# Four outer products of the squares in one joint tree: a bilinear kernel with a planned order

## The chip, the cores and the metric

The kernel runs on one core of a Trainium2 chip. The metric is the device time of one execution in microseconds (us), as the median of several runs. The core's engines work side by side and wait for each other by semaphores: TensorE (PE: matmuls from SBUF into PSUM), VectorE (DVE), ScalarE (ACT), GpSimd (POOL) and SyncE (SP, here only a queue for DMAs). ACT and POOL issue DMAs too; those that add onto their destination are POOL's.

## The reference

With x of 1024 x 512 and 64 embeddings, all in float32:

```python
out_lin = x @ lin_w.T + lin_b
xv = jnp.einsum('bf,efm->bem', x, weight)
zp = jnp.einsum('bf,efm->bem', jnp.square(x), jnp.square(weight))
y = out_lin + 0.5 * jnp.sum(jnp.square(xv) - zp, axis=1)
```

The sum over e of the second einsum is one product, of the squares of x (1024 x 512) with the squares of the weights summed over e (512 x 512).

## The kernel before, in words

**Tiling.** The model's 512 columns are worked in 16 groups of 32 (`group(g)`). A group is a product of x with a 512 x 2048 block of weights (32 columns times 64 embeddings). It is done by Strassen's scheme in Winograd's form on two levels: seven outer products (`ORDER`), each a `tree` of seven inner products. A product (`product`, L623) is two matmuls of 128x512 into the two banks of a PSUM tile. The inner sums of the weights (`t1` to `t4`) are POOL's; the outer sums T1 and T2 are built in memory, by a plain load and accumulating loads on POOL (`outer_sum`, `load_more`, L559). Of each tree, ACT copies three intermediate results out of PSUM or between PSUM tiles, DVE adds (L310), ACT squares (L324), DVE sums over the embeddings (L331). Outer product 4 is the sixth of a group and 3 the seventh; the text calls them tree 4 and tree 3. PSUM has four tiles of two banks: `b1`, `b3`, `b2_0`, `b2_1`.

**The squares.** The squares of x are made in groups 1 to 7 and parked in memory (`sq_dram`), with the sums of the inner level for outer products 1, 2, 5 and 6; the summed squares of the weights (`w2_sum`) grow with every group. Their product is made at the end: outer products 1, 2, 5 and 6 in inner trees, 7, 3 and 4 directly (`one_level`, L1083: the left operands are the plain loads raw7, raw3 and raw4). Its quarters go to the buffers v, o2, u2 and f, which are 256 columns wide in each of four positions.

- `twin_tree` makes two outer products side by side, one in each bank of a PSUM tile, with matmuls of 256 columns (L938). `first_twins` sets 1 and 2 ahead of tree 4 of the last group; the second pair, 6 and 5, is set behind tree 3.
- `preload` copies a sum of SBUF into a bank (ACT, L322), `one_level` adds a product onto it, `collect` adds the bank to one of the four blocks of the result (DVE, L1095). The blocks l11, l12, l21 and l22 hold the linear part, loaded by `lin_load` with accumulating loads of the interaction (L851).
- `add_to` (L824) adds v and o2 to l11 by accumulating DMAs on POOL. `turn` and `place` bring the last group's sums into rows (oa2), which `add_edge` adds to the result. `store` (L1036) writes the result, on SP's or ACT's queue, as the planner chooses.

**The order.** Nothing is issued as it is written: `Plan.add` records each step with its costs, reads and writes, and `Plan.order` emits all of them by a list schedule. TensorE's steps follow a fixed order by key (7 times the tree's number plus `PLACE`, so that neighbouring trees interleave); the others are taken by their latest times, with assumed costs, a hop of 0.3 us between engines and 0.05 on the same one. The names `b1`, `b3`, `b2_0`, `b2_1` stand for two banks each (`PAIRS`), which can be handed on one by one.

Of the kernel before, what the change touches and what calls it, by code (L numbers as in the profile page):

```python
# [29 lines left out]
class Plan:  # L30
# [11 lines left out]
    PAIRS = ("b1", "b3", "b2_0", "b2_1")  # L42
# [6 lines left out]
    def add(self, costs, emit, reads=(), writes=(), key=None, land=0.0,  # L49
# [7 lines left out]
            [m for n in names for m in (((n, 0), (n, 1)) if n in self.PAIRS else (n,))]  # L57
            for names in (reads, writes)
        )
        for r in reads:  # L60
            if r in self.writer:
                op.deps.add(self.writer[r])
# [11 lines left out]
    def order(self):  # L74
# [34 lines left out]
        def ready(o, e=None):  # L109
            at = self.HOP  # L110
            for d in o.deps:
                own = ops[d].engine == e and not ops[d].move
                at = max(at, ops[d].end + (self.OWN if own else self.HOP))
            return at
# [82 lines left out]
def kernel(  # L197
# [139 lines left out]
    def dma(o, i, reads, writes, move=1.75):  # L337
        plan.add({SP: 0.45}, lambda _: nc.sync.dma_start(o, i), reads, writes, land=2.0, move=move)
# [379 lines left out]
    def place(dst, b, names, writes, move):  # L718

        rows = dst.rearrange("m (n q b) -> q m n b", q=P // MG, b=MG)  # L720
        for q in range(P // MG):
            dma(rows[q], buf["turned"][ts(q, MG), b, :], names, (writes + (q,),), move)
# [78 lines left out]
    S = 7 * NG + 1  # L801
# [31 lines left out]

    def square_load(i):

        names = (f"R{i}", f"X{i}", f"Y{i}")
        dma(buf[f"X{i}"], sq_dram[:, i - 1], (("sqd", i),), names, 3.1)
# [84 lines left out]
    def twin_tree(at, b2, members):  # L922


        bank = {n: buf[n][:, :, 0:Q] for n in ("b1", "b3", b2)}
        side = {}
        for p, c in ((5, 0), (3, 1)):
            n = "wsq_1", c
            side[p] = buf["wsq_1"][:, c].rearrange("p (u b) -> p u b", u=2), n
            used("wsq_1", n, (n, 0), (n, 1))  # L930
        raw = all(src is None for _, src, _ in members)

        def product(p, b, first):
            for u, (i, _, _) in enumerate(members):
                op, names = tt[i][p]
                plan.add(
                    {PE: PAIR / 4},
                    lambda _, u=u, i=i, op=op: nc.tensor.matmul(  # L938
                        bank[b][:, u], op, buf[f"X{i}"][:, SLOT[p], :], start=first, stop=True,
                        skip_group_check=True,  # L940
                    ),
                    names + (f"{'Y' if p == 7 else 'X'}{i}", (b, u)), ((b, u),),
                    key=7 * at + PLACE[p] + 0.1 * u,
                )

        def aside(p, pos):
            o, n = side[p]
            act(o, bank["b3"], None, ("b3",), ((n, 0), (n, 1)), 0.65)
            for u, (_, src, _) in enumerate(members):
                if src:  # L950
                    costs, emit = two_input(POOL, o[:, u], o[:, u], part(src, pos), False, Q)
                    plan.add(costs, emit, ((n, u), (src, pos)), ((n, u),))

        def to(pos, b, p=None):

            if raw:
                q, c = divmod(pos, 2)
                o = buf[members[0][2][0]][:, :, c, ts(q, Q)]
                writes = tuple((dst, pos) for _, _, dst in members)
                if p is None:  # L960
                    act(o, bank[b], None, (b,), writes, 0.65)
                else:
                    plan.add(
                        {DVE: 0.62}, lambda _: nc.vector.tensor_add(o, bank[b], side[p][0]),
                        (b, (side[p][1], 0), (side[p][1], 1)), writes,
                    )
                return
            for u, (_, src, dst) in enumerate(members):
                if src is None and p is None:
                    act(part(dst, pos), bank[b][:, u], None, ((b, u),), ((dst, pos),), 0.4)  # L970
                    continue
                o, n = (side[p][0][:, u], (side[p][1], u)) if p else (part(src, pos), (src, pos))
                plan.add(
                    {DVE: 0.36},
                    lambda _, u=u, o=o, dst=dst: nc.vector.tensor_add(  # L975
                        part(dst, pos), bank[b][:, u], o
                    ),
                    ((b, u), n), ((dst, pos),),
                )

        product(5, "b3", True)
        aside(5, 3)
        product(3, "b3", False)
        aside(3, 1)
        product(1, "b1", True)
        act(bank[b2], bank["b1"], None, ("b1",), (b2,), 0.65)
        product(6, b2, False)
        to(1, b2, 3)
# [3 lines left out]
        to(3, b2, 5)  # L992
# [6 lines left out]
    def first_twins():  # L999
        halves_of(w(NG, "w22"))  # L1000
        halves_of("w12")
        lin_load(0, 0)
        for c in range(2):
            for z in range(2):
                halve(c, z)
        square_load(1)
        square_load(2)
        tt_at = w(NG, "w22"), 1
        w2_inner((1, 2), w2_sum.rearrange("p (r k) m -> p r k m", r=2)[:, :, :, 0:HM],
                 [("w2h", r, 0) for r in range(2)], tt_at,  # L1010
                 buf[tt_at].rearrange("p a n -> p (a n)"), *parts(tt_at))
# [4 lines left out]
        halves_of("T2")  # L1016
        used(*parts(tt_at), *((tt_at, "t", k, z) for k in range(1, 5) for z in range(2)))
        for block in ((1, 1), (0, 1), (1, 0)):
            lin_load(*block)
# [4 lines left out]
    def store(h, c, pos):  # L1024
# [10 lines left out]
        plan.add(  # L1035
            {SP: 0.45, ACT: 0.45}, lambda e: queues[e].dma_start(d, o),  # L1036
            tuple((n, z) for z in pos), (), land=2.0, move=0.44 * len(pos),
        )
# [17 lines left out]
    group(last, {5: first_twins})  # L1056


    raw = {}
    for i in (7, 3, 4):  # L1060
        n, at = f"raw{i}", {7: 7, 3: 1, 4: 2}[i]
        buf[n], raw[i] = block4(at), n
        used(f"X{at}", f"R{at}", f"Y{at}", n)
        dma(buf[n], sq_dram[:, i - 1, 0:4, :].rearrange("p (k q) b -> p k (q b)", k=2),
            (("sqd", i),), (n,))
    right = {7: (t_all[:, 2], "zt", 3), 4: (t_all[:, 3], "zt", 4), 3: (quad[1, 1], "w2h", 1, 1)}

    def bank_ap(bank):
        return buf[bank] if bank in buf else buf[bank[0]][:, bank[1], :]

    def preload(bank, src, u, lo, hi):
        here = tuple((src, pos) for pos in range(4) if pos % 2 == u and lo <= pos // 2 * Q < hi)
        act(bank_ap(bank)[:, 0:hi - lo], buf[src][:, u, lo:hi], None, here, (bank,),
            0.12 + 0.22 * (hi - lo) / Q)

    def one_level(i, bank, u, lo, hi, key):

        ap, *name = right[i]
        o = bank_ap(bank)[:, 0:hi - lo]

        def emit(_):
            for k in range(KH):
                nc.tensor.matmul(  # L1083
                    o, ap[:, k, ts(u, P)], buf[raw[i]][:, k, lo:hi], start=False, stop=k == 1,
                    skip_group_check=True,
# [5 lines left out]
    def collect(block, bank, u, lo, hi):  # L1091
        n = lin_all[block]
        here = tuple((n, pos) for pos in range(4) if pos % 2 == u and lo <= pos // 2 * Q < hi)
        d, o = buf[n][:, u, lo:hi], bank_ap(bank)[:, 0:hi - lo]
        plan.add({DVE: 0.08 + 0.28 * (hi - lo) / Q}, lambda _: nc.vector.tensor_add(d, d, o),  # L1095
                 here + (bank,), here)
        return here

    halves_of("T1")
    used("w11", *(("zt", k, z) for k in range(1, 5) for z in range(2)))  # L1100
    for z in range(2):
        w2_outer(z)
    w2_inner((5, 6), t_all[:, 0:2], [("zt", k) for k in (1, 2)], "wsq_0",
             buf["wsq_0"].rearrange("p a n -> p (a n)"))
    for i in (6, 5):
        square_load(i)
    b2 = b2_ring()
    upper = {u: (b2, u, "upper") for u in range(2)}
    for u, n in upper.items():
        buf[n] = buf[b2][:, u, Q:N]  # L1110
        used((b2, u), n)
    for q in range(2):
        for u in range(2):
            preload(upper[u], l21, u, q * Q, (q + 1) * Q)
            one_level(4, upper[u], u, q * Q, (q + 1) * Q, ((-0.6, -0.4), (9.5, 6.4))[q][u])
            act(part(l21, 2 * q + u), buf[upper[u]], None, (upper[u],), ((l21, 2 * q + u),), 0.34)
# [5 lines left out]
    for pos in (1, 3, 0, 2):  # L1122
        for o, a, b in ((v, u2, f), (l22, l22, f)):
            costs, emit = two_input(POOL, part(o, pos), part(a, pos), part(b, pos), False, Q)
            plan.add(costs, emit, ((a, pos), (b, pos)), ((o, pos),))
# [56 lines left out]
```

## Time and profile before

| | |
|---|---|
| median of 3 runs | 1409.11 us (1408.74 to 1409.27) |
| profiled execution, its own time | 1409.28 us |
| its span, first to last instruction | 1407.2 us |
| PE busy | 1398.1 us |
| DVE busy | 1094.7 us |
| POOL busy | 1043.1 us |
| ACT busy | 711.8 us |
| granted TensorE clock | 1.0 |

Times in the profile's rows are microseconds from the start of the span, means in the groups are nanoseconds. "Idle before" is how long an engine stood still ahead of a row, with what ended the wait. Each float32 matmul stands as two records, so a product of two matmuls is "x4". TensorE's ends are modelled; start to start is the safer reading. A DMA's row tells when it was issued; its landing stands apart, in the lists of DMAs.

### The profile page before, as it was taken

To read this page: it belongs to the slowest core of one execution; us is meant where nothing else is said; L and a number is where in the kernel's file an instruction comes from. 1 tells how busy PE (TensorE), PEld (TensorE's weight loads), DVE (VectorE), ACT (ScalarE), POOL (GpSimd) and SP (SyncE) were. 2 spreads that over 40 slices of the span, in tenths; PEclk is the share of its full clock that TensorE was granted. 3 is DMA by queue.
4 is the path that set the end of the run, shared out by engine and by line. 5 is a ranking of instruction groups with operands and counts; after the bars stand their busy time and mean duration, and the time that the engine had idled before them with its cause. 6 is when DMAs were issued, how large, how long until landed. Compare 5 with 4: busy or idle time off the path is not lost.

```text
span 1407.2 us, 10698 instructions
## 1 busy us (share of the span) xinstructions
PE 1398.1 (99%) x3308; PEld 628.9 (45%) x3308; DVE 1094.7 (78%) x976; ACT 711.8 (51%) x760; POOL 1043.1 (74%) x736
## 2 busy tenths in 40 slices
PE   9999999999999999999999999999999999999997
PEld 5444444444444444444444444444444444444454
DVE  7978696867969787795967869687795968869566
ACT  4545463544736456463544636454463644637334
POOL 5696776958678696776958678686777868679784
PEclk9999999999999999999999999999999999999999
DMA  6573564917649283573808447282663808447464
GB/s 224 165 190 120 134 183 116 249 53 189 214 106 236 88 226 125 146 213 101 221 30 197 135 116 187 60 241 61 159 174 90 213 30 208 125 120 183 107 177 108
DMA packets 55286, 211.84 MB, mean 151 GB/s; under 512 B 21504, under 2 KB 23296, under 8 KB 33344
## 3 DMA queue, kind: packets, MB, share of 16 engines
q0 software_dynamic: 12464, 83.76, 30.6%
q1 hardware_dynamic: 41200, 125.71, 25.2%
q10 hardware_dynamic: 1568, 1.71, 0.3%
q8 instruction: 27, 0.44, 0.1%
q14 instruction: 27, 0.22, 0.0%
HBM read 180.75 MB, written 12.45 MB: 137 GB/s over the span
## 4 chain that ended last, share of the span: by engine, by line
PE 98%; DMA 1%; DVE 0%; ACT 0%; issue 0%; ACTq 0%; SPq 0%; DVEq 0%
PE b L623 96%; PE b L456 1%; PE b L938 1%; PE b L1083 1%; DMA oa<-xT 0%; DMA ob<-lin_wT 0%; ACT b L322 0%; DVE T L975 0%; DVE w22a L1095 0%; ACT T L322 0%; DVE x_all L310 0%; ACTq L356 0%; DVE T L1095 0%; SPq L349 0%; ACT ob L324 0%
## 5 line engine op out<-in xcount | busy, mean ns | idle before, releaser
L623 PE MATMUL b<-t,x_all 128*128 128x512 f32 x1792 | 806.2, 592 | 0.0
L623 PEld LDWEIGHTS b<-t,x_all 128*128 128x128 f32 x1792 | 340.5, 190 | 425.6 <-issue 419.5
L623 PE MATMUL b<-w,x_all 128*128 128x512 f32 x768 | 358.1, 592 | 0.0
L310 POOL TENSOR_TENSOR t<-w 128x512 f32<-128x512 f32 x128 | 174.3, 1362 | 154.8 <-PE b L623 85.0
L322 ACT COPY p<-b 128x1024 f32<-128x1024 f32 x161 | 161.8, 1005 | 159.6 <-PE b L623 159.5
L623 PEld LDWEIGHTS b<-w,x_all 128*128 128x128 f32 x768 | 145.9, 190 | 182.9 <-issue 171.7
L310 POOL TENSOR_TENSOR t<-w,t 128x512 f32<-128x512 f32 x128 | 176.4, 1378 | 60.4 <-PE b L623 60.4
L324 ACT ACTIVATE oa<-oa 128x1024 f32<-128x1024 f32 x124 | 129.7, 1057 | 142.6 <-DVE oa L310 142.5
L623 PE MATMUL b<-T,x_all 128*128 128x512 f32 x384 | 180.4, 592 | 0.0
L331 DVE TENSOR_REDUCE acc<-oa 128x16 f32<-128x1024 f32 x124 | 148.9, 1211 | 37.9 <-ACT oa L324 37.9
L322 ACT COPY b<-b 128x1024 f32<-128x1024 f32 (+1 forms) x114 | 113.0, 992 | 119.8 <-PE b L623 119.4
L331 DVE TENSOR_REDUCE w_sum<-wsq 128x16 f32<-128x1024 f32 x128 | 154.1, 1206 | 12.5 <-ACT wsq L324 12.5
L310 DVE TENSOR_TENSOR oa<-b,p 128x1024 f32<-128x1024 f32 x95 | 115.8, 1219 | 38.9 <-PE b L623 38.8
L324 ACT ACTIVATE wsq<-w 128x1024 f32<-128x1024 f32 x96 | 98.2, 1056 | 67.8 <-DVE w_sum L331 67.8
L310 POOL TENSOR_TENSOR t<-T 128x512 f32<-128x512 f32 x64 | 90.3, 1411 | 56.6 <-issue 33.2
L324 ACT ACTIVATE c<-c 128x1024 f32<-128x1024 f32 x77 | 79.4, 1057 | 77.5 <-POOL c L310 51.7
L623 PEld LDWEIGHTS b<-T,x_all 128*128 128x128 f32 x384 | 73.0, 190 | 91.8 <-issue 91.6
L310 DVE TENSOR_TENSOR p<-b,p 128x1024 f32<-128x1024 f32 x79 | 96.2, 1218 | 18.0 <-PE b L623 17.9
L310 DVE TENSOR_TENSOR ob<-b,p 128x1024 f32<-128x1024 f32 x48 | 58.6, 1221 | 66.3 <-PE b L623 66.2
L310 POOL TENSOR_TENSOR t<-T,t 128x512 f32<-128x512 f32 x64 | 81.6, 1275 | 17.3 <-PE b L623 17.2
L310 POOL TENSOR_TENSOR c<-oa,p 128x1024 f32<-128x1024 f32 x32 | 88.9, 2778 | 0.0
L310 POOL TENSOR_TENSOR ob<-ob,p 128x1024 f32<-128x1024 f32 x32 | 88.8, 2786 | 0.0
(104 smaller groups left out, 1405.0 us busy)
## 6 DMA issues: line engine op xcount, KB each, us to landing
w<-weight SPq DMA_DIRECT2D x48, 1024.0 KB, 5.0
T<-weight POOLq DMA_DIRECT2D x45, 1024.0 KB, 8.5
T<-weight SPq DMA_DIRECT2D x30, 1024.0 KB, 6.9
w<-weight POOLq DMA_DIRECT2D x16, 1024.0 KB, 11.2
w<-T POOLq DMA_DIRECT2D x16, 1024.0 KB, 7.0
w22a<-weight SPq DMA_DIRECT2D x8, 1024.0 KB, 6.6
w22b<-weight SPq DMA_DIRECT2D x8, 1024.0 KB, 6.8
c<-xT SPq DMA_DIRECT2D x9, 512.0 KB, 5.4
```

Source lines behind the costliest of these rows:

```text
L310: f(o, a, b)
L322: nc.scalar.copy(o, i)
L324: nc.scalar.activation(o, i, func)
L331: lambda _: nc.vector.tensor_reduce(o, i.rearrange("p a (m e) -> p a m e", e=E), axis=AX.X, op=ALU.add),
L456: nc.tensor.matmul(buf[bank][:, c, rows], b[:, k, ts(c, P)], a[:, k, rows], start=first and k == 0 and rows.start == 0, stop=k == KH - 1, ...
L623: nc.tensor.matmul(buf[b][:, j, :], buf[f"X{i}"][:, SLOT[p], ts(j, P)], op, start=first, stop=True, skip_group_check=True,)
L938: lambda _, u=u, i=i, op=op: nc.tensor.matmul(bank[b][:, u], op, buf[f"X{i}"][:, SLOT[p], :], start=first, stop=True, skip_group_check=True,),
L1083: nc.tensor.matmul(o, ap[:, k, ts(u, P)], buf[raw[i]][:, k, lo:hi], start=False, stop=k == 1, skip_group_check=True,)
```

## The change

All four inner trees of the squares become one `joint_tree`, set ahead of tree 3 of the last group: each product has four matmuls of 256 columns, outer products 1 and 2 in one bank and 6 and 5 in the other. The additions and copies out of it are 128x512 wide, for two outer products at once. The sums of v, o2, u2 and f are 16 POOL additions; o2 takes v in, so that one accumulating DMA to l11 remains of two; oa0 takes u2 + f as the source for product 3. The one-level products are wider, two banks' halves at most, and 4 follows 7 in the same bank. The operands of the squares get other places (5 in X7, raw7 in X5, raw4 in X4, raw3 in oa1). Of the edge rows' DMAs and the stores, `dma(..., on=(SP, ACT))` lets the planner choose the queue.

In `Plan`, a PSUM tile is one unit, a reader of it counts as a writer, and TensorE's own hop is 0. This reorders steps of DVE, ACT and POOL in all groups.

```diff
-    PAIRS = ("b1", "b3", "b2_0", "b2_1")
+    PSUM = ("b1", "b3", "b2_0", "b2_1")
         reads, writes = (
-            [m for n in names for m in (((n, 0), (n, 1)) if n in self.PAIRS else (n,))]
+            [n[0] if isinstance(n, tuple) and n[0] in self.PSUM else n for n in names]
             for names in (reads, writes)
         )
+        writes += [n for n in reads if n in self.PSUM and n not in writes]
...
-                at = max(at, ops[d].end + (self.OWN if own else self.HOP))
+                at = max(at, ops[d].end + (self.OWN * (e != PE) if own else self.HOP))
...
-    def dma(o, i, reads, writes, move=1.75):
-        plan.add({SP: 0.45}, lambda _: nc.sync.dma_start(o, i), reads, writes, land=2.0, move=move)
+    def dma(o, i, reads, writes, move=1.75, on=(SP,)):
+        plan.add(dict.fromkeys(on, 0.45), lambda e: queues[e].dma_start(o, i), reads, writes,
+                 land=2.0, move=move)
...
-    S = 7 * NG + 1
+    S = 7 * NG
...
+    square_at = {1: 1, 2: 2, 6: 6, 5: 7}
...
-    def twin_tree(at, b2, members):
...
+    def joint_tree(at, members):
+        b2, p5, p53 = b2_ring(), p5_ring(), p53_ring()
+        def product(p, b, first):
+            def emit(_):
+                for z, (i, _) in enumerate(members):
+                    u, lo = z // 2, z % 2 * Q
+                    nc.tensor.matmul(
+                        buf[b][:, u, lo:lo + Q], tt[i][p][0], buf[f"X{square_at[i]}"][:, SLOT[p], :],
+                        start=first and not lo, stop=True, skip_group_check=True,
+                    )
...
+            plan.add({PE: PAIR}, emit, names + x + (b,), (b,), key=7 * at + PLACE[p])
+        def to(pos, b, p=None):
+            q, c = divmod(pos, 2)
+            for u in range(2):
+                here = [dst for _, dst in members[2 * u:2 * u + 2]]
+                o = buf[here[0][0]][:, :, c, ts(q, Q)]
+                i = buf[b][:, u, :].rearrange("p (z b) -> p z b", b=Q)
...
+                if p is None:
+                    act(o, i, None, (b,), writes, 0.57)
+                else:
...
+                        {DVE: 0.62}, lambda _, o=o, i=i, a=a: nc.vector.tensor_add(o, i, a),
...
         product(5, "b3", True)
-        aside(5, 3)
+        act(buf[p5], buf["b3"], None, ("b3",), (p5,))
         product(3, "b3", False)
-        aside(3, 1)
+        act(buf[p53], buf["b3"], None, ("b3",), (p53,))
         product(1, "b1", True)
-        act(bank[b2], bank["b1"], None, ("b1",), (b2,), 0.65)
+        act(buf[b2], buf["b1"], None, ("b1",), (b2,))
...
-    def first_twins():
...
-        twin_tree(S - 3, b2_ring(), ((1, None, v), (2, None, o2)))
-        add_to(l11, v)
+    def squares_tree():
...
+        joint_tree(S - 1, ((1, v), (2, o2), (6, u2), (5, f)))
+        in_parts("oa0")
+        for pos in (1, 0, 3, 2):
+            for n, a, b in ((o2, o2, v), (u2, u2, v), (l22, l22, f), ("oa0", u2, f)):
+                costs, emit = two_input(POOL, part(n, pos), part(a, pos), part(b, pos), False, Q)
+                plan.add(costs, emit, ((a, pos), (b, pos)), ((n, pos),))
         add_to(l11, o2)
         store(0, 0, every)
...
-    group(last, {5: first_twins})
+    group(last, {6: squares_tree})
...
-    twin_tree(S, b2, ((6, v, u2), (5, None, f)))
     for h in (1, 0):
         b, names = turn(last, 1 + h, h == 1)
-        place(buf["oa2"][P - MG:P, h, :], b, names, ("edge", h), 0.0)
+        place(buf["oa2"][P - MG:P, h, :], b, names, ("edge", h), 0.0, (SP, ACT))
     add_edge(1)
...
+    b2 = [b2_ring(), b2_ring()]
+    for u, bank in ((1, b2[0]), (0, "b3")):
+        o = buf[bank][:, u, :]
+        preload(bank, o, u2, u, 0, H)
+        for i, h, key in ((7, 1, 6.5), (4, 0, 10)):
+            one_level(i, bank, o, u, 0, H, key + 3 * (1 - u))
+            if i == 7 and not u:
+                act(buf[u2][:, u, :], o, None, (bank,), here(u2, u, 0, H), 0.56)
+                add_row(l22, u2, u)
+            else:
+                collect((1, i == 7), bank, o, u, 0, H)
+            store(1, i == 7, (u, 2 + u))
+    for u, lo, hi, bank, key in ((1, 0, H, "b1", 9.7), (0, 0, Q, b2[1], 14), (0, Q, H, b2[0], 15)):
+        o = buf[bank][:, 0, 0:hi - lo]
+        preload(bank, o, "oa0", u, lo, hi)
+        one_level(3, bank, o, u, lo, hi, key)
+        names = collect((0, 1), bank, o, u, lo, hi)
+        if u:
+            add_edge(0)
+        store(0, 1, tuple(pos for _, pos in names))
```

More of the change, by code (lines that the diff above doesn't have):

```diff
@@ L716, in turn, with place @@
         return b, names
-    def place(dst, b, names, writes, move):
+    def place(dst, b, names, writes, move, on=(SP,)):
         rows = dst.rearrange("m (n q b) -> q m n b", q=P // MG, b=MG)
         for q in range(P // MG):
-            dma(rows[q], buf["turned"][ts(q, MG), b, :], names, (writes + (q,),), move)
+            dma(rows[q], buf["turned"][ts(q, MG), b, :], names, (writes + (q,),), move, on)
     def x_squares(i):
@@ L832, in add_row @@
         plan.add(costs, emit, rows, rows[:2], both=engine == DVE)
+    square_at = {1: 1, 2: 2, 6: 6, 5: 7}
     def square_load(i):
-        names = (f"R{i}", f"X{i}", f"Y{i}")
-        dma(buf[f"X{i}"], sq_dram[:, i - 1], (("sqd", i),), names, 3.1)
+        at = square_at[i]
+        names = (f"R{at}", f"X{at}", f"Y{at}")
+        dma(buf[f"X{at}"], sq_dram[:, i - 1], (("sqd", i),), names, 3.1)
     def lin_load(h, c):
@@ L920, in w2_inner @@
             }
-    def twin_tree(at, b2, members):
[L925 to L931, printed above, removed]
-        def product(p, b, first):
[L934 to L952, printed above, removed]
-        def to(pos, b, p=None):
[L956 to L959, printed above, removed]
@@ new lines, in joint_tree @@
+    def joint_tree(at, members):
+        b2, p5, p53 = b2_ring(), p5_ring(), p53_ring()
+        def product(p, b, first):
+            def emit(_):
[5 more added lines that the diff above has]
+                    )
+            names = tuple(n for i, _ in members for n in tt[i][p][1])
+            x = tuple(f"{'Y' if p == 7 else 'X'}{square_at[i]}" for i, _ in members)
+            plan.add({PE: PAIR}, emit, names + x + (b,), (b,), key=7 * at + PLACE[p])
+        def to(pos, b, p=None):
+            q, c = divmod(pos, 2)
[3 more added lines that the diff above has]
+                i = buf[b][:, u, :].rearrange("p (z b) -> p z b", b=Q)
+                writes = tuple((dst, pos) for dst in here)
@@ L960, in to @@
                 if p is None:
-                    act(o, bank[b], None, (b,), writes, 0.65)
+                    act(o, i, None, (b,), writes, 0.57)
                 else:
+                    a = buf[p][:, u, :].rearrange("p (z b) -> p z b", b=Q)
                     plan.add(
-                        {DVE: 0.62}, lambda _: nc.vector.tensor_add(o, bank[b], side[p][0]),
-                        (b, (side[p][1], 0), (side[p][1], 1)), writes,
-                    )
[L967 to L979, printed above, removed]
+                        {DVE: 0.62}, lambda _, o=o, i=i, a=a: nc.vector.tensor_add(o, i, a),
+                        (b, p), writes,
+                    )
@@ L981, in twin_tree @@
         product(5, "b3", True)
[L982 removed]
+        act(buf[p5], buf["b3"], None, ("b3",), (p5,))
         product(3, "b3", False)
[L984 removed]
+        act(buf[p53], buf["b3"], None, ("b3",), (p53,))
         product(1, "b1", True)
[L986 removed]
+        act(buf[b2], buf["b1"], None, ("b1",), (b2,))
         product(6, b2, False)
[L988 removed]
+        to(1, b2, p53)
         product(2, "b1", False)
@@ L991, in twin_tree @@
         product(7, b2, False)
-        to(3, b2, 5)
+        to(3, b2, p5)
         product(4, b2, False)
@@ L997 @@
     v, o2, u2, f = ("w12", 0), ("w12", 1), ("T1", 0), ("T1", 1)
-    def first_twins():
-        halves_of(w(NG, "w22"))
-        halves_of("w12")
-        lin_load(0, 0)
+    def squares_tree():
+        for n in (w(NG, "w22"), "w12", "T1", "T2"):
+            halves_of(n)
+        used("w11", *(("zt", k, z) for k in range(1, 5) for z in range(2)))
         for c in range(2):
@@ L1005, in first_twins @@
                 halve(c, z)
-        square_load(1)
-        square_load(2)
-        tt_at = w(NG, "w22"), 1
-        w2_inner((1, 2), w2_sum.rearrange("p (r k) m -> p r k m", r=2)[:, :, :, 0:HM],
-                 [("w2h", r, 0) for r in range(2)], tt_at,
-                 buf[tt_at].rearrange("p a n -> p (a n)"), *parts(tt_at))
-        twin_tree(S - 3, b2_ring(), ((1, None, v), (2, None, o2)))
-        add_to(l11, v)
+        for i in (1, 2, 6, 5):
+            square_load(i)
+        for z in range(2):
+            w2_outer(z)
+        flat = [buf[f"wsq_{z}"].rearrange("p a n -> p (a n)") for z in range(2)]
+        w2_inner((1, 2), w2_sum.rearrange("p (r k) m -> p r k m", r=2)[:, :, :, 0:HM],
+                 [("w2h", r, 0) for r in range(2)], "wsq_1", flat[1])
+        w2_inner((5, 6), t_all[:, 0:2], [("zt", k) for k in (1, 2)], "wsq_0", flat[0])
+        for block in blocks:
+            lin_load(*block)
+        joint_tree(S - 1, ((1, v), (2, o2), (6, u2), (5, f)))
[4 more added lines that the diff above has]
+                plan.add(costs, emit, ((a, pos), (b, pos)), ((n, pos),))
         add_to(l11, o2)
         store(0, 0, every)
[L1016 to L1019, printed above, removed]
     every = (0, 1, 2, 3)
@@ L1034, in store @@
             o, d = part(n, pos[0]), out_dst[:, 2 * c + u, lo + q * Q:lo + (q + 1) * Q]
[L1035 to L1038, printed above, removed]
+        dma(d, o, tuple((n, z) for z in pos), (), 0.44 * len(pos), (SP, ACT))
     def add_edge(h):
@@ L1054, in add_edge, with here, in_rows, preload @@
             )
-    group(last, {5: first_twins})
[L1059 to L1073, printed above, removed]
+    def here(n, u, lo, hi):
+        return tuple((n, pos) for pos in range(4) if pos % 2 == u and lo <= pos // 2 * Q < hi)
+    def in_rows(o, ap):
+        return ap.rearrange("p (q b) -> p q b", b=Q) if len(o.shape) == 3 else ap
+    def preload(bank, o, src, u, lo, hi):
+        act(o, in_rows(o, buf[src][:, u, lo:hi]), None, here(src, u, lo, hi), (bank,),
             0.12 + 0.22 * (hi - lo) / Q)
-    def one_level(i, bank, u, lo, hi, key):
+    def one_level(i, bank, o, u, lo, hi, key, first=False):
         ap, *name = right[i]
-        o = bank_ap(bank)[:, 0:hi - lo]
         def emit(_):
@@ L1083, in emit @@
                 nc.tensor.matmul(
-                    o, ap[:, k, ts(u, P)], buf[raw[i]][:, k, lo:hi], start=False, stop=k == 1,
-                    skip_group_check=True,
+                    o, ap[:, k, ts(u, P)], in_rows(o, buf[raw[i]][:, k, lo:hi]),
+                    start=first and k == 0, stop=k == 1, skip_group_check=True,
                 )
@@ L1089, in one_level, with collect @@
                  tuple((*name, z) for z in range(2)) + (raw[i], bank), (bank,), key=7 * S + key)
-    def collect(block, bank, u, lo, hi):
+    def collect(block, bank, o, u, lo, hi):
         n = lin_all[block]
-        here = tuple((n, pos) for pos in range(4) if pos % 2 == u and lo <= pos // 2 * Q < hi)
-        d, o = buf[n][:, u, lo:hi], bank_ap(bank)[:, 0:hi - lo]
+        names = here(n, u, lo, hi)
+        d = in_rows(o, buf[n][:, u, lo:hi])
         plan.add({DVE: 0.08 + 0.28 * (hi - lo) / Q}, lambda _: nc.vector.tensor_add(d, d, o),
-                 here + (bank,), here)
-        return here
@@ L1099 @@
[L1099 to L1116, printed above, removed]
@@ L1117 @@
-    twin_tree(S, b2, ((6, v, u2), (5, None, f)))
+                 names + (bank,), names)
+        return names
+    group(last, {6: squares_tree})
+    raw = {7: "raw7", 3: "oa1", 4: "raw4"}
+    for i in (7, 4, 3):
+        if i != 3:
+            at = {7: 5, 4: 4}[i]
+            buf[raw[i]] = block4(at)
+            used(f"X{at}", f"R{at}", f"Y{at}", raw[i])
+        dma(buf[raw[i]], sq_dram[:, i - 1, 0:4, :].rearrange("p (k q) b -> p k (q b)", k=2),
+            (("sqd", i),), (raw[i],))
@@ L1118 @@
+    right = {7: (t_all[:, 2], "zt", 3), 4: (t_all[:, 3], "zt", 4), 3: (quad[1, 1], "w2h", 1, 1)}
     for h in (1, 0):
         b, names = turn(last, 1 + h, h == 1)
-        place(buf["oa2"][P - MG:P, h, :], b, names, ("edge", h), 0.0)
+        place(buf["oa2"][P - MG:P, h, :], b, names, ("edge", h), 0.0, (SP, ACT))
     add_edge(1)
[L1122 to L1125, printed above, removed]
@@ L1126 @@
-    b2 = b2_ring()
-    for u in (1, 0):
-        preload((b2, u), u2, u, 0, H)
-    for u in (1, 0):
-        one_level(7, (b2, u), u, 0, H, 11 - u)
-        for h, c in ((1, 0), (1, 1)):
-            if u and not c:
-                act(buf[u2][:, u, :], buf[b2][:, u, :], None, ((b2, u),), ((u2, 1), (u2, 3)), 0.56)
-                add_row(l21, u2, u)
-            else:
-                collect((h, c), (b2, u), u, 0, H)
-            store(h, c, (u, 2 + u))
-    for u in (1, 0):
-        for q, bank in enumerate((("b3", u), ("b1", u))):
-            preload(bank, v, u, q * Q, (q + 1) * Q)
-            one_level(3, bank, u, q * Q, (q + 1) * Q, 14 - 2 * u + q)
-            collect((0, 1), bank, u, q * Q, (q + 1) * Q)
+    b2 = [b2_ring(), b2_ring()]
@@ L1143 @@
+    for u, lo, hi, bank, key in ((1, 0, H, "b1", 9.7), (0, 0, Q, b2[1], 14), (0, Q, H, b2[0], 15)):
[3 more added lines that the diff above has]
+        names = collect((0, 1), bank, o, u, lo, hi)
         if u:
             add_edge(0)
-        for q in range(2):
-            store(0, 1, (2 * q + u,))
+        store(0, 1, tuple(pos for _, pos in names))
     for op, engine in plan.order():
```

## The prediction

> **What bounds the kernel now.** I read the page's head and its chain first, then TensorE's waits, then TensorE's rows in order of time over the last 65 us.
>
> ```profile
> span 1407.2 us, 10698 instructions
> PE 1398.1 (99%) x3308; PEld 628.9 (45%) x3308; DVE 1094.7 (78%) x976; ACT 711.8 (51%) x760; POOL 1043.1 (74%) x736
> ...
> PE 98%; DMA 1%; DVE 0%; ACT 0%; issue 0%; ACTq 0%; SPq 0%; DVEq 0%
> ...
> L623 PE MATMUL b<-t,x_all 128*128 128x512 f32 x1792 | 806.2, 592 | 0.0
> ```
>
> TensorE is the bound: 98% of the chain, and its main rows have 0.0 idle before them. The granted clock is 1.0, so nothing is to be had there. A change can only win where TensorE stands still, and these rows hold nearly all of that (columns: start, length, operation, idle before it and what ended it):
>
> ```profile
> 1351.50 1.13 PE L938 MATMUL b<-x_all,w_sum 128*128 128x256 f32 x4
> 1352.47 3.60 PE L623 MATMUL b<-t,x_all 128*128 128x512 f32 x8
> ...
> 1384.27 1.88 PE L623 MATMUL b<-t,x_all 128*128 128x512 f32 x4
> 1386.67 1.13 PE L938 MATMUL b<-x_all,wsq 128*128 128x256 f32 x4 [0.52 <-ACT b L322]
> 1387.64 1.03 PE L938 MATMUL b<-x_all,w 128*128 128x256 f32 x4
> 1388.81 1.13 PE L938 MATMUL b<-x_all,wsq 128*128 128x256 f32 x4 [0.15 <-DVE T L975]
> 1389.78 1.03 PE L1083 MATMUL b<-x_all,w 128*128 128x256 f32 x4
> 1391.75 1.10 PE L938 MATMUL b<-x_all,wsq 128*128 128x256 f32 x4 [0.94 <-DVE T L975]
> 1392.69 2.74 PE L1083 MATMUL b<-x_all,w 128*128 128x256 f32 x8
> 1396.11 1.98 PE L1083 MATMUL b<-x_all,w 128*128 128x512 f32 x4 [0.68 <-ACT b L322]
> 1397.93 1.89 PE L1083 MATMUL b<-x_all,w_sum 128*128 128x256 f32 x8
> 1401.19 1.99 PE L1083 MATMUL b<-x_all,w_sum 128*128 128x256 f32 x8 [1.37 <-DVE T L1095]
> ```
>
> A product of two 512-column matmuls takes 1.72 us start to start, a 256-column pair 0.86. What each start is later than that is lost: 0.11 (1352.47), 0.68, 0.11, 0.31, 0.11, 1.11, 0.08, 0.84 (after a 256 pair and a 512 pair, 2.58), 0.10, 1.54, and 0.10 in the last row. Sum 5.09 us; the printed idle is 3.66, the rest is the first matmul after a stop (1.13 instead of 1.03). The reason is visible: after 1385 only the second twin tree and the one-level products are left, each waiting for a copy or addition of the step just before, with nothing to put between.
>
> After the last matmul (1403.18) come an addition, a store and the end: 4.0 us.
>
> ```profile
> 1402.22 1.79 ACTq L1036 DMA_DIRECT2D out<-T  x3
> ...
> 1403.22 0.42 DVE L1095 TENSOR_TENSOR T<-T,b 128x256 f32<-128x256 f32 x1 [0.44 <-PE b L1083]
> ```
>
> **The change part by part.**
> *Products.* 28 matmuls of 256 columns stay 28, the one-level products keep their columns: all matmuls together stream 831,232 columns in both programs. TensorE's work changes by 0; six matmuls fewer only means longer ones.
>
> *Where they stand.* This is the gain. The joint tree's seven products (four matmuls, 1.72 each) are interleaved one for one with products of trees 4 and 3, so each handoff of a bank has a 1.72 us product of another tree in its cover; tree 3's last products then cover the first one-level products. Counting back from an unbroken end, E = 1403.18 - 5.09 = 1398.09, the new order's last products start at: joint product 7 at about 1375.6, 4 at 1379.0; tree 3's last four from 1380.7 to 1387.6, with the first one-level product (raw7) among them at 1385.9; raw7 again 1389.3, raw3 1391.1, raw4 1392.8 and 1394.5, raw3's halves 1396.2 and 1397.1.
> Handoffs, by durations of the trace: joint product 7 to 4 needs two DVE additions of 128x512 (0.69, started 0.60 apart: 1.3) under one 1.72 product, 0.3 to spare. The tree's usual addition of 128x1024 (1.22) stands under 1.72, as in every group now. Copies into a bank (0.59) for raw7 need T1's sums: four POOL additions per quarter at 0.73, 16 in all, 11.7 us between 1373 and 1385; the first copy is free about 1382.6, 3 us early. So TensorE's stops go: -5.1.
>
> *PSUM tiles as units.* A reader or writer now takes both banks. [...] I take 0.2 for the closest.
>
> *Order in all groups.* The unit rule and TensorE's zero own-hop also reorder DVE, ACT and POOL in every group (TensorE's order is the same up to the last tree 5). Mostly an addition and a reduction change places, 1.2 us each; the rows of TensorE show 0.0 idle, and the handoffs that free a bank keep their places among themselves. Gain 0, as nothing is lost there. The one step with DMAs: POOL's second accumulating load of T moves behind two 1024-wide additions. Now:
>
> ```profile
> 681.82 1.17 POOL L559 DMA_DIRECT2D T<-weight  x1
> 682.42 2.96 POOL L310 TENSOR_TENSOR ob<-ob,p 128x1024 f32<-128x1024 f32 x1
> 684.74 2.95 POOL L310 TENSOR_TENSOR c<-oa,p 128x1024 f32<-128x1024 f32 x1
> ...
> 694.32 1.83 POOL L310 TENSOR_TENSOR t<-T 128x512 f32<-128x512 f32 x1
> ```
>
> It is issued at 686.4 instead of 681.8; at the median 8.5 us of its row it lands at 694.9, 0.6 after its reader. TensorE reads that t only at 706.0, and the addition of ob that DVE waits for in each group (732.20, 2.46 idle) ends 3.5 us before TensorE needs the bank. Cost 0, bounds below.
>
> *ACT's queue.* Before, all of ACT's six stores stand behind its last copy (1398.99 on). Now ten issues stand among its copies: four edge rows that were SP's, and the 512 KB store of l11, which waits for POOL's accumulating DMA of o2. Behind it wait two edge rows and the copy into the bank of the very last matmul pair. [...] POOL issues that DMA at about 1387.2 (its sums end at 1384.9, one addition of 2.35 follows). The two rows of its kind:
>
> ```profile
> L824 POOL DMA_DIRECT2D w22a<-w x1: 902/902/902, 1365.6 to 1365.6; - x1
> ...
> DMA to landing us min/median/max: 9.4/9.4/9.4
> ```
>
> and the one at 1376.92, which took 6.5 (the upper figure of the three for its stretch):
>
> ```profile
> L824 POOL DMA_DIRECT2D w22a<-w x1: 1198/1198/1198, 1376.9 to 1376.9; - x1
> ...
> DMA to landing us min/median/max: 4.2/5.3/6.5
> ```
>
> The 9.4 ran beside three plain loads of 512 KB; at 1387 none is left, so 6.5 is nearer: landed at 1393.7. DVE's turn of the sums, which the edge rows need anyhow, ends at 1394.5 (addition at 1389.5, three reductions of 1.13, transpose 0.3), so the store holds nobody. The copy then runs at 1395.4 and is needed at 1397.0. [...]
>
> *The end.* The edge addition on DVE (0.69) now stands between the last two collections: the last addition ends 0.1 later after E than now. The edge rows may land in 2.7 instead of 1.8 us (their own rows' extremes), since a 512 KB store goes just ahead: then 0.5 more. I take both, 0.6.
>
> *Sum.* -5.1 + 0.2 + 0.6 = -4.3. The profiled execution took 1409.28 us for a span of 1407.2; 1409.28 - 4.3 = 1405.0. The median of the three runs is 0.17 lower, so 1404.8.
>
> **The rivals.**
> *1, ACT held by the accumulating DMA.* At 9.4 us it lands at 1396.6; store and two edge issues (0.45 each) put the copy's end at 1398.35, TensorE's last pair 1.3 to 1.4 late; the edge rows land at 1399.4, the edge addition and the last one end at 1400.5 instead of 1398.65: 1.9 lost, gain 2.4, time 1406.7. For it: the row of 9.4. Against: no load runs beside it. It would eat the whole gain only from about 12 us.
> *2, the groups stall (slower).* The mechanism is the moved load of T. Later than its reader by the 3.5 us of cover and about 1 us of POOL's own gaps, that is from 12.5 us to landing, every further microsecond stops TensorE once in each of 15 groups. From 0.3 us beyond, 4.3 is gone; at 1 us beyond the time is 1409.1 - 4.3 + 15 = about 1420. For it: these loads now overlap the next group's plain loads, and the longest in the trace took 11.8. Against: median 8.5, and the load ahead of it in its queue has landed by 687.8.
> *3, half of it.* Handoffs with 0.2 to 0.3 to spare are missed repeatedly, or more products than I see wait for POOL: half of 5.1 comes back as other stops, end as above: gain 1.8, time 1407.3.
> *4, nothing moves.* The planner fails to cover: 1409. The order, read product by product, speaks against it.
>
> **How the numbers follow.** Forecast 1404.8: 0.62. Rival 1: 0.13. Rival 3: 0.14. Rival 4: 0.03. Rival 2: 0.08. Without the 0.8 of small losses the time is 1403.9; below that lies little. The range 1403.8 to 1408.2 leaves out rival 2, most of rival 4 and little below. Some 0.2% (2.8 us) is what a measurement of this kernel can tell from no change. Faster by more, under 1406.3: the forecast, and of rivals 1 and 3 a third each: 0.71. Within: the other two thirds of these and rival 4, 0.21. Slower: rival 2, 0.08.
>
> **What would show it.** Right: TensorE's rows after 1342 with no idle over 0.2, the last matmul ending near 1398.3; the accumulating DMA of o2 landing under 8 us; ACT's last copy under 1396; POOL's wait for T under 1 us a group. Wrong: an idle above 0.5 before the last pair released by ACT (rival 1), any idle at the trees' line in the groups (rival 2), stops released by DVE or POOL after 1350 (rival 3).

## The result and the profile after

The kernel after took 1403.66 us (median of 6 runs, 1402.97 to 1405.15); the kernel before, in the same session, 1409.26 (6 runs, 1408.74 to 1409.55). The ratio is 0.9962, with a 95% interval of 0.9949 to 0.9974: faster by 5.6 us where 4.3 had been forecast. The profiled execution took 1404.54 us for a span of 1402.7.

The head of the page, and the start of its chain:

```profile
span 1402.7 us, 10645 instructions
PE 1396.1 (100%) x3296; PEld 626.6 (45%) x3296; DVE 1093.5 (78%) x971; ACT 711.5 (51%) x748; POOL 1050.2 (75%) x741
...
PE 98%; DMA 1%; DVE 0%; ACTq 0%; SPq 0%; DVEq 0%; issue 0%
```

TensorE is the bound as before. It streams the same columns (831,232 by the traces of both); what went is time in which it stood. Its rows in order of time over the stretch that held the stops, the joint products in L936, tree 3 in L625 and the one-level products in L1055:

```profile
1376.37 1.89 PE L936 MATMUL b<-x_all,wsq 128*128 128x256 f32 x8
1378.10 1.88 PE L625 MATMUL b<-w22b,x_all 128*128 128x512 f32 x4
1379.81 1.89 PE L936 MATMUL b<-x_all,wsq 128*128 128x256 f32 x8
1381.54 1.88 PE L625 MATMUL b<-t,x_all 128*128 128x512 f32 x4
1383.26 1.88 PE L625 MATMUL b<-w22b,x_all 128*128 128x512 f32 x4
1384.97 1.88 PE L625 MATMUL b<-t,x_all 128*128 128x512 f32 x4
1386.69 1.88 PE L1055 MATMUL b<-x_all,w 128*128 128x512 f32 x4
1388.40 1.88 PE L625 MATMUL b<-t,x_all 128*128 128x512 f32 x4
1390.12 1.88 PE L1055 MATMUL b<-x_all,w 128*128 128x512 f32 x4
1391.84 1.88 PE L1055 MATMUL b<-oa,w_sum 128*128 128x512 f32 x4
1393.56 3.60 PE L1055 MATMUL b<-x_all,w 128*128 128x512 f32 x8
1396.99 1.89 PE L1055 MATMUL b<-oa,w_sum 128*128 128x256 f32 x8
```

No row of this stretch shows an idle, and none the 0.1 us of a restart (by the rows of before, a pair of 256 columns took 1.10 to 1.13 us after a stop and 1.03 otherwise): each product starts 1.72 us after the one before it (a row of x8 and 3.60 holds two of them, the last row two halves). TensorE's waits over the whole span say the same: there are three, 1.3, 0.8 and 0.7 us, and all of them lie in the first 17 us.

The end, on DVE and SP's queue:

```profile
1398.05 0.42 DVE L1067 TENSOR_TENSOR T<-T,b 128x256 f32<-128x256 f32 x1 [0.18 <-PE b L1055]
1398.50 0.69 DVE L1034 SCALAR_TENSOR_TENSOR T<-oa,T 32x512 f32<-32x512 f32 x1
1399.22 0.42 DVE L1067 TENSOR_TENSOR T<-T,b 128x256 f32<-128x256 f32 x1
1399.67 0.34 SPq L339 DMA_DIRECT2D out<-T  x1
```

The last matmul ends at 1398.88 (1396.99 + 1.89), the span 3.9 us later; it was 4.0 before.

**An account that leaves the start out.** The first product of the trees starts between 27.63 and 28.74 us in the six profiles of this document, and the latest of them is this one: TensorE waited 1.32 us for a load of x (at 7.04), and by 12.30 it is 0.84 behind the kernel before. So both kernels are measured from the same product, the first of the first tree (`b<-t,x_all`, at 27.92 before and at 28.74 after). The page gives the spans to a tenth; the table has them from the trace to the hundredth, 1407.17 and 1402.75.

| profiled execution, us | before | after | difference |
|---|---|---|---|
| first product of the trees | 27.92 | 28.74 | +0.82 |
| from there to the end of the last matmul | 1375.26 | 1370.14 | -5.12 |
| from there to the end of the span | 3.99 | 3.87 | -0.12 |
| outside the span (own time less span) | 2.11 | 1.79 | -0.32 |
| its own time | 1409.28 | 1404.54 | -4.74 |

Without the row of the start the gain is 5.56 us, the same size as the 5.6 of the medians. No profile shows what lies outside the span; why it is 0.32 shorter is open.

### The profile page after: what moved, and what is told of

Read it like the earlier page. It is cut to its first block, busy times and chain, and to the rows that moved or that the text cites. A ratio compares the mean times of both kernels' runs of the same rounds, so it can differ in the third digit from the quotient of the medians.

```text
span 1402.7 us, 10645 instructions
## 1 busy us (share of the span) xinstructions
PE 1396.1 (100%) x3296; PEld 626.6 (45%) x3296; DVE 1093.5 (78%) x971; ACT 711.5 (51%) x748; POOL 1050.2 (75%) x741
## 4 chain that ended last, share of the span: by engine, by line
PE 98%; DMA 1%; DVE 0%; ACTq 0%; SPq 0%; DVEq 0%; issue 0%
PE b L625 96%; PE b L458 1%; PE b L936 1%; PE b L1055 1%; DMA ob<-lin_wT 0%; DMA oa<-xT 0%; DVE x_all L311 0%; ACTq L358 0%; SPq L351 0%; DVE T L1034 0%; DVEq L1138 0%; DVE T L1067 0%; DVEq L311 0%
## 5 line engine op out<-in xcount | busy, mean ns | idle before, releaser
L625 PE MATMUL b<-t,x_all 128*128 128x512 f32 x1792 | 806.0, 592 | 0.0
L625 PEld LDWEIGHTS b<-t,x_all 128*128 128x128 f32 x1792 | 340.4, 190 | 427.0 <-issue 420.7
L625 PE MATMUL b<-w,x_all 128*128 128x512 f32 x768 | 358.1, 592 | 0.0
L625 PEld LDWEIGHTS b<-w,x_all 128*128 128x128 f32 x768 | 145.9, 190 | 183.7 <-issue 182.5
L311 POOL TENSOR_TENSOR t<-w,t 128x512 f32<-128x512 f32 x128 | 175.3, 1370 | 56.7 <-PE b L625 56.5
L625 PE MATMUL b<-T,x_all 128*128 128x512 f32 x384 | 180.4, 592 | 0.0
L323 ACT COPY b<-b 128x1024 f32<-128x1024 f32 x113 | 112.7, 997 | 133.0 <-PE b L625 132.5
L311 POOL TENSOR_TENSOR t<-T 128x512 f32<-128x512 f32 x64 | 86.4, 1350 | 56.6 <-issue 30.9
L625 PEld LDWEIGHTS b<-T,x_all 128*128 128x128 f32 x384 | 73.0, 190 | 91.8 <-issue 90.9
L311 POOL TENSOR_TENSOR c<-oa,p 128x1024 f32<-128x1024 f32 x32 | 84.7, 2647 | 0.0
L311 DVE TENSOR_TENSOR oa<-b,oa 128x1024 f32<-128x1024 f32 x62 | 75.6, 1219 | 9.5 <-PE b L625 9.5
## 6 DMA issues: line engine op xcount, KB each, us to landing
w22a<-weight SPq DMA_DIRECT2D x8, 1024.0 KB, 10.9
w22b<-weight SPq DMA_DIRECT2D x8, 1024.0 KB, 10.9
```

The costliest lines, as they stand in the source:

```text
L311: f(o, a, b)
L323: nc.scalar.copy(o, i)
L625: nc.tensor.matmul(buf[b][:, j, :], buf[f"X{i}"][:, SLOT[p], ts(j, P)], op, start=first, stop=True, skip_group_check=True,)
```

## The experiments

All four go by the medians of one session, in which the kernel before had 1409.22 (27 runs); the kernel after stands with the 1403.66 of the result.

### The planner's rules alone, and the tree alone

The change has two halves that could each have moved time: the planner's rules, which reorder the four other engines in all groups, and the joint tree with what belongs to it. The first two kernels have one each. For `plan_only` the rules were put into the kernel before, and held to the steps of the groups, since TensorE's fixed order at the twin trees doesn't agree with whole tiles:

```diff
+    unit = True
...
+        if self.unit:
+            writes = writes + [n for n in reads if n[0] in self.PAIRS and n not in writes]
...
-                at = max(at, ops[d].end + (self.OWN if own else self.HOP))
+                at = max(at, ops[d].end + (self.OWN * (e != PE) if own else self.HOP))
...
     def first_twins():
+        plan.unit = False
...
+        plan.unit = True
...
     group(last, {5: first_twins})
+    plan.unit = False
```

> The kernel before with the planner's new rules alone, in the steps of the groups: a reader of a PSUM tile counts as a writer, TensorE's own hop is 0. TensorE's order is that of before, instruction for instruction; some 530 places in the orders of the other four engines change to those of the kernel after. Theory (the gain is TensorE's stops behind 1385, and nothing in the groups waits): 1409.2 +- 0.4, with the stops of before at the twin trees, 5.1 us in all. Rival (the order in the groups brought part of it): 1407 or less. Rival 2 of the prediction (the moved load of T costs): above 1410.

Measured: 1408.95 us (11 runs, 1408.64 to 1409.52), ratio 0.9999 (0.999 to 1.0007). TensorE's five stops are those of before, to the hundredth; the longest three of its rows:

```profile
...
1391.46 1.10 PE L941 MATMUL b<-x_all,wsq 128*128 128x256 f32 x4 [0.94 <-DVE T L978]
1395.82 1.98 PE L1089 MATMUL b<-x_all,w 128*128 128x512 f32 x4 [0.68 <-ACT b L325]
1400.90 1.99 PE L1089 MATMUL b<-x_all,w_sum 128*128 128x256 f32 x8 [1.37 <-DVE T L1101]
```

`tree_only` is the kernel after with the planner's rules of before:

```diff
-    PSUM = ("b1", "b3", "b2_0", "b2_1")
+    PAIRS = ("b1", "b3", "b2_0", "b2_1")
...
-            [n[0] if isinstance(n, tuple) and n[0] in self.PSUM else n for n in names]
+            [m for n in names for m in (((n, 0), (n, 1)) if n in self.PAIRS else (n,))]
...
-        writes += [n for n in reads if n in self.PSUM and n not in writes]
...
-                at = max(at, ops[d].end + (self.OWN * (e != PE) if own else self.HOP))
+                at = max(at, ops[d].end + (self.OWN if own else self.HOP))
```

> The kernel after with the planner's old rules (two banks handed on one by one, own hop 0.05): the joint tree alone. TensorE's order is that of after; the groups' order on the other engines is that of before. Theory: as after, 1403.7 +- 0.7, no idle of TensorE over 0.2 behind 1342. If the order in the groups had a part, it lies between, 1405 or more.

Measured: 1403.95 us (5 runs, 1403.51 to 1404.03), ratio 0.9962 (0.9948 to 0.9975), the same as after. From the first product of the trees (28.16) to the end of the last matmul (1396.42 + 1.89) it takes 1370.15 us; after takes 1370.14.

So the whole gain is the tree's, with what belongs to it (the wider one-level products, the 16 sums, the choice of queues: these were not run apart), and the rules are worth nothing here, in either company. The new order in the groups costs nothing either: `plan_only` has the moved load of T in its groups, as after has.

### The joint tree behind the last tree

Is it that the tree is joint, or where its products stand? `joint_late` keeps the joint tree and sets it where the second twin tree was, behind tree 3:

```diff
-        joint_tree(S - 1, ((1, v), (2, o2), (6, u2), (5, f)))
+        joint_tree(S, ((1, v), (2, o2), (6, u2), (5, f)))
...
-                 tuple((*name, z) for z in range(2)) + (raw[i], bank), (bank,), key=7 * S + key)
+                 tuple((*name, z) for z in range(2)) + (raw[i], bank), (bank,), key=7 * S + key + 4)
...
-    group(last, {6: squares_tree})
+    group(last)
+    squares_tree()
```

> The kernel after with the joint tree set behind tree 3, its one-level products later still: joint, but in the place of the second twin tree. Theory (the gain is cover, not the joint form): product 7 to 4 of the joint tree has no product of tree 3 left between and waits 1.8 us for two additions; the one-level products wait 1.7 us more for POOL's 16 sums of 0.73. TensorE stands still for 3.5 to 3.8 us, the end is up to 0.7 longer: 1407.3 to 1408.2. Rival (the joint form is what counts): within 1 us of after, 1403.7 to 1404.7.

Measured: 1406.88 us (10 runs, 1406.55 to 1407.59), ratio 0.9984 (0.9975 to 0.9993): 3.2 us above after. TensorE's rows in order of time:

```profile
1384.00 1.89 PE L936 MATMUL b<-x_all,wsq 128*128 128x256 f32 x8
1387.51 1.99 PE L936 MATMUL b<-x_all,wsq 128*128 128x256 f32 x8 [1.63 <-DVE T L958]
1389.49 1.98 PE L1055 MATMUL b<-x_all,w 128*128 128x512 f32 x4
1393.01 1.98 PE L1055 MATMUL b<-x_all,w 128*128 128x512 f32 x4 [1.54 <-ACT b L323]
```

The two stops are the two that were expected. Joint product 7 (1384.00) and product 4 (1387.51) stand next to each other, with two additions between; DVE set a transpose between the two (1386.58), which put the second 0.2 us later. The second stop is a copy into the bank that waits itself for POOL's sums (ACT at 1392.37, 1.20 idle, released by POOL's addition of T).

Start to start TensorE loses 1.79, 0.26, 1.80 and 0.11, in sum 3.96, a little above the 3.8 that was expected at most; the stretch from the first tree to the last matmul is 1374.09 us, 3.95 above after. The time is 0.4 below what was expected all the same, since the end came 0.4 shorter than in after, where it was expected longer. With tree 3 done early, the edge addition is out of the way before the last collections: DVE does it at 1397.53. The last addition starts at 1401.91, 0.04 after the last matmul, here, and 0.34 after it in the kernel after, where the edge addition is in its way.

A joint tree in the old place keeps 2.3 us of the gain and loses the rest to handoffs without cover. (A handoff is the step between two products in one bank: the copy or additions that must be done before the second may start. Its cover is the foreign product that TensorE works on meanwhile.)

### The joint tree in its place, in one piece

`joint_apart` leaves the tree ahead of tree 3 and takes the interleaving away: its seven products follow each other.

```diff
-            plan.add({PE: PAIR}, emit, names + x + (b,), (b,), key=7 * at + PLACE[p])
+            plan.add({PE: PAIR}, emit, names + x + (b,), (b,), key=7 * at + 0.1 * (5, 3, 1, 6, 2, 7, 4).index(p))
```

> The kernel after with the seven joint products in one piece, ahead of tree 3's products 3 to 4, in the order 5, 3, 1, 6, 2, 7, 4: same place as after, no interleaving. Theory (each handoff needs a foreign product of 1.72 us in its cover): stops of 1.27 (copy p5 to product 3), 1.26 (copy to product 6), 1.55 (additions to product 4) and 1.26 (the same copy in tree 3, whose cover went too), 5.3 in all, and 0.1 a restart: 1408.8 to 1409.3, all of the gain gone though the tree is joint and ahead. Rival (the queue of work ahead of the last tree is long enough whatever the order): 1404.5 or less.

Measured: 1410.29 us (10 runs, 1409.78 to 1410.94), ratio 1.0009 (0.9999 to 1.0018): the gain is gone to the last microsecond, and it may be slower than before. TensorE's waits after 1355:

```profile
1364.49 1.13 PE L936 MATMUL b<-x_all,w_sum 128*128 128x256 f32 x4 [1.10 <-ACT p L323]
1369.30 1.99 PE L936 MATMUL b<-x_all,wsq 128*128 128x256 f32 x8 [1.09 <-ACT b L323]
...
1372.86 1.89 PE L936 MATMUL b<-x_all,wsq 128*128 128x256 f32 x8
1376.13 1.99 PE L936 MATMUL b<-x_all,wsq 128*128 128x256 f32 x8 [1.38 <-DVE T L958]
...
1381.39 3.60 PE L625 MATMUL b<-w22b,x_all 128*128 128x512 f32 x8
1386.16 1.96 PE L625 MATMUL b<-t,x_all 128*128 128x512 f32 x4 [1.18 <-ACT b L323]
```

Four stops at the four expected places, released by the copies and additions that were named. Start to start they are 1.27, 1.25, 1.55 and 1.33, and the restarts 0.11, 0.11, 0.11 and 0.08: 5.81 in all, and 1375.93 us from the first tree to the last matmul, 5.79 above after. The fourth belongs to tree 3: the joint products that had covered its copy are no longer there.

The time is 1.0 above the upper expectation. Of that 0.1 is in the stops, and 0.1 is that the expectation's own terms (5.3, and 0.1 for each of four restarts) add up to 1409.4. Most of the rest is the end: its last store is issued right behind the last addition, as in after, but lands after 3.0 us and not 2.2 (the DMA issues of its last 10 us, with KB each and us to landing; then the share of the DMA engines in use, in tenths, in 40 slices of 0.05 us from 1405.2 to 1407.2, and that stretch's load of instructions, with its packets, MB and share):

```profile
out<-T SPq DMA_DIRECT2D x1, 128.0 KB, 3.0
...
DMA  9597997898999640000000000000000100000000
...
q14 instruction: 1, 0.01, 3.0%
```

By the trace's packets, 135 of the store's 144 are over by 1406.01. The other nine, one sixteenth, begin at 1406.67, just as a load of 8 KB of instructions ends that had begun at 1405.72. In after the load nearest the end ran at 1395.40, ahead of the last stores. So a load of instructions most likely held a sixteenth of the store; whether it does so in each of the ten runs isn't known.

## Why the prediction was right, point by point

The direction and the mechanism were right, and the gain of 5.1 us on TensorE to the tenth. The two losses that were set against it did not come, so 1403.66 lies 0.14 us under the range that was given, 1403.8 to 1408.2.

**Bound and mechanism.** TensorE is the bound and only its stops can be won. `joint_apart` shows it from the other side: the same products, columns and additions as in after, with stops put back, take 1410.29 us.

**Where they stand (-5.1).** Measured from the first tree to the last matmul: -5.12. The sum of the start-to-start excesses was the right measure; the printed idle alone (3.66) would have come out 1.5 short. Less the 0.82 of the late start, the last products begin where they had been counted back to, within 0.1 (joint product 4 at 1378.99 for 1379.0, the last halves at 1396.17 for 1396.2). That neither the joint form nor the place is enough without the cover is shown by `joint_late` and `joint_apart`; the edit of the latter changes nothing but the order of TensorE's products, and the stops come back where a handoff loses its foreign product. Whether twin trees ahead of tree 3, interleaved as closely, would do as well was not run.

**PSUM tiles as units (+0.2): mis-sized, 0.** The 0.2 was the author's estimate, and no run shows it: in after the product of the closest handoff, joint product 4 at 1379.81, starts on time, 1.71 us after the one before it. `joint_apart` gives the size of this handoff, since there nothing covers it: 1.55 us. Under 1.72 that leaves 0.17 to spare, where the prediction had 0.3. It was read a little too wide and held all the same; in after the second addition ends at 1379.58 (1378.90 + 0.68), 0.23 before product 4 starts, where without cover 0.06 lay between the two (1376.07 and 1376.13 in `joint_apart`). `tree_only`, with banks handed on singly elsewhere, gains nothing. The joint products themselves take both banks in either kernel, so handing on single banks was not run at this handoff; by the rows both banks' additions fit under one product, and it had nothing to win.

**Order in all groups (0).** Right, by `plan_only`. The moved load of T does what was said. POOL's rows in the group shown:

```profile
687.27 1.17 POOL L561 DMA_DIRECT2D T<-weight  x1
...
695.31 1.29 POOL L561 DMA_DIRECT2D T<-weight  x1
696.37 1.54 POOL L311 TENSOR_TENSOR t<-T 128x512 f32<-128x512 f32 x1
```

Its landing is listed at 9.0 us after the issue, so it lands at 696.3 and its reader starts 0.1 later. Before, the load was issued at 681.82, took 10.9 and left its reader 1.6 us. So POOL now does wait for the load, in each of groups 2 to 15 by matching loads and readers: by its rows for up to 0.6 us, in two groups for 1.2 and 1.3, so that the sign "under 1 us a group" was missed in two of 14. The row's "idle before" doesn't print it here, since another DMA issue stands in between. TensorE's rows in the groups show no idle, so the cover swallows it. That the wait came near the 0.6 that was forecast is in part luck: the 8.5 us was the median of a row that mixes three loads of each group, while this one had taken 10.6 to 11.3 us in every one of these groups; at its new time it happened to take 8.7 to 9.9. How far the cover reaches, that is the 12.5 us of rival 2, wasn't run and stays a reading.

**ACT's queue (0).** Right, with room. The accumulating DMA of o2 took 4.5 us, less than the 6.5 and 9.4 of the rows that were weighed, and the store behind it held nobody:

```profile
L826 POOL DMA_DIRECT2D w22a<-w x1: 884/884/884, 1388.0 to 1388.0; - x1
...
DMA to landing us min/median/max: 4.5/4.5/4.5
```

```profile
1392.59 0.40 ACTq L339 DMA_DIRECT2D out<-w22a  x1
...
1395.30 1.51 ACTq L339 DMA_DIRECT2D oa<-turned  x2
1396.86 0.38 ACT L323 COPY b<-oa 128x256 f32<-128x256 f32 x1 [3.47 <-DVE T L1067]
```

It lands at 1392.5 and ACT issues the store at once. The sign "last copy under 1396" was missed, at 1396.86. Of this 0.82 is the late start; but the copy is still 0.6 later than the 1395.4 that had been worked out. Two things hold it, and they end within 0.05 us of each other: DVE's collection out of its bank (until 1396.76), and ACT's own two issues of edge rows, which took 0.61 and 0.87 (until 1396.81) where 0.45 each had been assumed. The copy is done at 1397.24, before the half at 1397.85 that needs it. Rival 1 thus did not occur. That a DMA of 9.4 us would have held ACT, and with it the copy behind the store, was not run.

**The end (+0.6): the step that was mis-sized, -0.12.** Both parts of it were off. The edge rows landed after 1.8 us on SP's queue and 2.1 on ACT's, not 2.7: the 512 KB store had been issued 2.7 us before them. The edge addition does delay the last addition, by 0.3 and not 0.1 (0.34 after the last matmul, against 0.04 in before). But the last store goes out on SP's queue the moment that addition ends, and the span ends 3.11 us behind it (1402.75 - 1399.64), against 3.53 before (1407.17 - 1403.64).

The store has no part in this gain: from issue to landing it took 2.16 us in after (1399.67 to 1401.84) and 1.86 in before (1403.68 to 1405.54). What is shorter is the piece behind the landing, 0.91 for 1.63. There SyncE closes the program with nine waits for semaphores, 0.06 us apart where nothing holds them. Its waits for stores (total in us, times, longest), before and after:

```profile
SPq L1178 <- DMA out<-T: 2.9, 1, 2.9
...
SPq L1138 <- DMA out<-T: 1.4, 3, 0.5
```

In before the second of the nine is for the store that lands last, and the seven behind it run only then (1405.62 to 1406.01). In after it is the ninth that is for that store, and the other eight are done by its landing. That is 0.43 of the 0.72; the other 0.29 is a pause of POOL before it clears the semaphores (0.32 in before, 0.03 in after), whose cause is open. The prediction had not looked at this piece; that it came out shorter is luck.

**The sum.** Forecast -4.3 from -5.1, +0.2 and +0.6; measured, from the first product of the trees on, -5.12, 0 and -0.12, with -0.32 outside the span: -5.56. The range reached down to 1403.8. With both losses at 0 the prediction's own sum is 1404.0 (1409.1 - 5.1; it writes 1403.9). A shorter end and less time outside the span were not in it, and these two brought the time below the range.

**The rivals.** 3, half of the gain lost to missed handoffs, is what `joint_late` became: stops that wait for DVE and for POOL's sums, 2.3 us of gain left. In the kernel after it did not happen, with 0.17 us to spare. 4 is refuted by the rows.

## What to carry to other kernels

When one engine is the bound, add up how much later than its work each instruction starts, not the idle that is printed, and ask of each handoff which foreign work stands in its cover and by how much it is longer. The same products cost TensorE 5.8 us more through their order alone (`joint_apart` against after); that joining the trees was needed for enough foreign work to stand between is argued from the order, not run. An order changed on engines that aren't waited for was worth nothing here: more than 500 moved places in `plan_only` (564 in the trace, by operation and buffers) changed the time by less than its interval. And the end of a program has a piece of its own behind the last landing, which a forecast of tenths has to read too.

## What the runs showed of the hardware that was not expected

- The start is where these profiles differ. The six reach the first product of the trees between 27.63 us (`plan_only`) and 28.74 (after), and from there to the last matmul `plan_only` repeats before, and `tree_only` repeats after, within 0.01 us over more than 1370, though the other engines' order is not the same. A small change on TensorE is better read from such a stretch of one profile than from few medians.
- An accumulating DMA of 512 KB took 4.5 to 9.4 us in these traces: 4.5 in after and `tree_only`, 4.7 in `joint_late`, 6.2 in `joint_apart`, 6.5 and 9.4 before, 6.7 and 9.2 at the same two places in `plan_only`. So it goes with the place in the program, within 0.2 us; a row from one place is a poor estimate for another, and the 4.5 lies below both rows that the prediction had.
- The piece behind the last landing was 1.63 us in before and `plan_only`, and 0.91 in after, `tree_only`, `joint_late` and (0.90) `joint_apart`. Of this 0.43 goes with which of SyncE's closing waits is for the store that lands last.
